# Four layers of cross attention on one core: last block projected into rows, its last sums on TensorE, small inputs fetched another way

## The chip, the cores and the metric

The kernel runs on one core of a Trainium2 chip. The metric is the device time of one execution in microseconds (us); before the change it was 4903.22 us, the median of three runs that lie between 4901.65 and 4903.43.

## The reference, cut to what matters

A sequence `x` of 2048 rows of 256 values goes through four layers of cross attention to the same context of 1601 rows of 512 values. Everything is float32. Layers 0, 2 and 3 are "masked" layers of 16 heads of 64 values; layer 1 is a grouped layer with an RMS norm ahead of it, which the change does not touch. A masked layer is, in the reference's words:

```python
q, k, v = hidden @ Wq, ctx @ Wk, ctx @ Wv            # 16 heads of 64
logits = einsum('bhqd,bhkd->bhqk', q, k) * 64 ** -0.5
col_bias[:, token_indices_A] = (-20.0 * (1 - mask_A))[:, None]
col_bias[:, token_indices_B] = (-20.0 * (1 - mask_B))[:, None]
out = softmax(logits + col_bias) @ v
hidden = out @ Wo + bo + hidden
```

`mask_A` and `mask_B` have one value for each of the 2048 rows, the token indices two values each, `bo` 256 values.

## The kernel before, in words

**Tiling.** A masked layer is done in 8 blocks of two heads. A block is done in four units, one for each quarter `b` of the rows (512 rows). A unit takes the context in 13 chunks of 128 positions (the last has 65); a step of the main loop (L1145) is one chunk. `x` is held transposed in `xs`: 256 columns as two groups of 128 partitions, rows along the free dimension.

**A unit.** Per chunk, TensorE makes the scores of both heads (L687) in a pair of PSUM banks, of which there are two (`psum.pair`), ScalarE copies them to SBUF (L699) and VectorE keeps a running maximum (L702, L704). After 13 chunks the maximum is turned (L747, L748), sent through DRAM to all partitions, and copied into a third PSUM pair `b` (L763). A unit later, per chunk, VectorE adds it (L768), ScalarE takes the exponential (L773), GpSimd adds the exponentials up in `sums` (a copy for chunk 0, L776, then twelve additions, L778), and TensorE multiplies them with the values (L813) into `po`, which ScalarE copies to `oT` (L818). Three pieces of work follow: `denominators` (L824) turns `sums` with eight transposes (L834), reduces (L838) and takes the reciprocal (L839), and sends the result through DRAM to all partitions as `by` (L655, L658); `divide` (L853) multiplies `oT` by it on GpSimd; `project` (L856) multiplies with `Wo` (L862) and adds to `xs` (L874), in the last block of a layer with the bias `bo` as well (L869). In the last block of the last layer `rows_out` (L626) then turns the quarter of `xs` back into rows with eight transposes (L631), copies it with ScalarE and VectorE, half each (L634, L635), and asks for two output transfers (L637).

**Order.** TensorE, ScalarE and VectorE run in the order in which the program is written (L1196 to L1202 make that binding). GpSimd and SyncE run in an order that the tile scheduler makes. Where the three pieces of a unit come is set by steps: `finish` (L876) gives the distance in steps from the unit's last chunk (2 or 3 for the denominators, 5 for the division, 10 for the projection), `after` (L1049) adds `rows_out` at 11. Projections of keys and values for the next block fill the steps between; in the last block there are none.

**Start.** `token_numbers` (L142) fetches twelve token indices, each to all 128 partitions, in six transfers of two values. Some 25 small VectorE instructions (`key_order`, L159) work out from them in which order the context rows are taken, and 13 indirect transfers of GpSimd gather the rows (L258). TensorE meanwhile turns `x` (L592) and makes the first queries (L464). `masks_parts` (L298) fetches both masks with row `n * 128 + p` on partition `p`, and the masks become bias rows later (L306 and on). `small_constants` (L370) fetches the biases `bo` and the norm's weights, value by value onto partitions, on GpSimd's queue; it is written at step 14 of the first unit, and the scheduler puts its requests at the start.

Of the kernel before, what the change touches and what calls it, by code (L numbers as in the profile page):

```python
# [10 lines left out]
FP = mybir.dt.float32  # L11
BF = mybir.dt.bfloat16
I32 = mybir.dt.int32
AF = mybir.ActivationFunctionType
ALU = mybir.AluOpType
# [3 lines left out]
P = 128  # L19
QB = 512  # L20
# [6 lines left out]
Piece = namedtuple("Piece", "run cost shared", defaults=(True,))  # L27
# [7 lines left out]
def tile_cross_attention_stack(ctx: ExitStack, tc: tile.TileContext, t: dict, out: bass.AP):  # L35
# [31 lines left out]
    nc = tc.nc  # L67
    x, cond = t["x"], t["ctx_2048"]
    _, S, C = x.shape
    _, T, CT = cond.shape  # L70
    NQ = S // P
    NC = C // P
    NCT = CT // P
    NB = S // QB
    QT = QB // P
    TCH = spans(T, P)
    NT = len(TCH)
# [3 lines left out]
    masked_names = ["L0_xattn_", "L2_xattn_", "L3_xattn_"]  # L81

    NP = 22
    const = ctx.enter_context(tc.tile_pool(name="const", bufs=1))
    weights = ctx.enter_context(tc.tile_pool(name="weights", bufs=2))
    heads = ctx.enter_context(tc.tile_pool(name="heads", bufs=2))
    probs = ctx.enter_context(tc.tile_pool(name="probs", bufs=NP))
    work = ctx.enter_context(tc.tile_pool(name="work", bufs=2))
    small = ctx.enter_context(tc.tile_pool(name="small", bufs=2))
    dram = ctx.enter_context(tc.tile_pool(name="dram", bufs=1, space=bass.MemoryType.DRAM))  # L90
    ps_o = ctx.enter_context(tc.tile_pool(name="ps_o", bufs=1, space=PSUM))
    ps_m = ctx.enter_context(tc.tile_pool(name="ps_m", bufs=1, space=PSUM))
    scores_pools = ctx.enter_context(ExitStack())

    ident = const.tile([P, P], FP, name="ident")
    make_identity(nc, ident)
    ones = const.tile([P, P], FP, name="ones")
# [32 lines left out]
    psum = Scores()  # L130
# [3 lines left out]
    xs = const.tile([P, NB, NC, QB], FP, name="xs")  # L134
# [5 lines left out]
    NTOK = 4 * NL  # L140

    def token_numbers():  # L142

        idx = const.tile([P, NTOK], I32, name="tok_idx")
        for l, name in enumerate(masked_names):
            for s, which, queue in ((0, "A", nc.sync), (2, "B", nc.scalar)):
                queue.dma_start(
                    out=idx[:, 4 * l + s : 4 * l + s + 2],
                    in_=t[name + "token_indices_" + which]
                    .rearrange("(o s) -> o s", o=1).to_broadcast((P, 2)),  # L150
                )
        tok = const.tile([P, NTOK], FP, name="tok")
        nc.vector.tensor_copy(tok, idx)
        wrap = small.tile([P, NTOK], FP, name="wrap", bufs=1)
        nc.vector.tensor_scalar(wrap, tok, 0.0, float(T), ALU.is_lt, ALU.mult)
        nc.vector.tensor_tensor(tok, tok, wrap, ALU.add)
        return tok
# [138 lines left out]
        nc.vector.tensor_copy(put(2), rest)  # L296

    def masks_parts():  # L298
        masks = probs.tile([P, 2, NQ], FP, name="p")
        with nc.allow_non_contiguous_dma(reason="2048 values of a mask, once"):  # L300
            nc.sync.dma_start(out=masks[:, 0, :], in_=t["mask_S_fk1"].rearrange("(n p) -> p n", p=P))
            nc.sync.dma_start(out=masks[:, 1, :], in_=t["mask_S_fk0"].rearrange("(n p) -> p n", p=P))
        parts = const.tile([P, 6, NQ], FP, name="mask_parts")

        def make():
            nc.vector.tensor_scalar(masks, masks, -1.0, 1.0, ALU.mult, ALU.add)  # L306
            nc.vector.tensor_scalar(masks, masks, -SUPPRESS, None, ALU.mult)
            for m in range(2):
                three_parts(masks[:, m, :], [NQ], lambda i: parts[:, 3 * m + i, :])

        return parts, make
# [52 lines left out]
    bo_of = []  # L364
# [5 lines left out]
    def small_constants():  # L370
        with nc.allow_non_contiguous_dma(reason="columns of 256 values"):
            for name in masked_names:
                bo_of.append(const.tile([P, NC], FP, name="bo_" + name))
                nc.gpsimd.dma_start(out=bo_of[-1], in_=t[name + "bo"].rearrange("(k p) -> p k", p=P))
            nc.gpsimd.dma_start(out=normw, in_=t["L1_xattn_norm_w"].rearrange("(k p) -> p k", p=P))
        nc.gpsimd.memset(sel, 0.0)
        for h, r in enumerate(QUARTERS):
            nc.gpsimd.tensor_copy(den_rows[:, h : h + 1], ident[:, r + 16 : r + 17])
            nc.gpsimd.tensor_copy(
                sel[:, :, h, :16], ident[:64, :64].rearrange("p (g d) -> p g d", d=16)  # L380
            )
        nc.vector.tensor_reduce(one_row, den_rows, AX.X, ALU.add)
# [240 lines left out]
            (12, Piece(rms, 1.5)),  # L623
        ]

    def rows_out(b):  # L626

        pt = psum.pair((QT, C))
        for q in range(QT):
            for k in range(NC):  # L630
                nc.tensor.transpose(pt[:, q, ts(k, P)], xs[:, b, k, ts(q, P)], ident)  # L631
        rows = work.tile([P, QT, C], FP, name="ct", bufs=3)
        half = QT // 2
        nc.scalar.copy(rows[:, :half, :], pt[:, :half, :])  # L634
        nc.vector.tensor_copy(rows[:, half:, :], pt[:, half:, :])  # L635
        for q0 in (0, half):
            nc.sync.dma_start(  # L637
                out=out[0, b * QB + q0 * P : b * QB + (q0 + half) * P, :].rearrange(
                    "(n p) c -> p n c", p=P
                ),  # L640
                in_=rows[:, q0 : q0 + half, :],
            )

    def columns(q):

# [15 lines left out]
    class Unit:  # L661
        def __init__(self, l, u, b, sub):
            self.l, self.u, self.b, self.sub = l, u, b, sub
            self.layer = u.layer
            self.pair = self.layer.SUBS[sub]
            self.masked = isinstance(self.layer, Masked)
            self.p = [None] * NT

        def rows(self, h):
            size = P // len(self.pair)  # L670
# [99 lines left out]
        def masked_exp(self, c):  # L770
            m = TCH[c][1]
            p = self.p[c]
            nc.scalar.activation(p[:m], p[:m], AF.Exp)  # L773
            if c == 0:
                self.sums = work.tile([P, 2, QB], FP, name="sums")
                nc.gpsimd.tensor_copy(self.sums, p)  # L776
            else:
                nc.gpsimd.tensor_tensor(self.sums[:m], self.sums[:m], p[:m], ALU.add)  # L778

        def scores_again(self, c, h, s):  # L780
# [17 lines left out]
        def values(self, c, part=None):  # L798


            u = self.u
            _, m = TCH[c]
            if c == 0 and not part:
                self.po = ps_o.tile([P, QB], FP, name="po")
            for h in range(len(self.pair)):
                r = self.rows(h)
                if self.masked:
                    to, v, p = self.po[r, :], u.v[:m, c, r], self.p[c][:m, h, :]
                else:
                    at = ts(part, QB // 2)  # L810
                    to, v = self.po[r, at], u.v[:m, c, :]
                    p = self.p[c][h // 2][:m, h % 2, at]
                nc.tensor.matmul(  # L813
                    to, v, p, start=(c == 0 and not part), stop=(c == NT - 1 and part != 0)
                )
            if c == NT - 1 and part != 0:
                self.oT = work.tile([P, QB], FP, name="oT", bufs=1)
                nc.scalar.copy(self.oT, self.po)  # L818

        @property  # L820
# [35 lines left out]
        def project(self):  # L856

            k = 0
            for py in psum.heads(False):
                of = range(k, k + py.shape[1])  # L860
                for k in of:
                    nc.tensor.matmul(  # L862
                        py[:, k - of[0], :], self.u.wo[:, ts(k, P)], self.oT, start=True, stop=True
                    )
                k += 1
                if self.masked and self.u.n == self.layer.BLOCKS - 1:
                    for j in of:
                        bo, to = bo_of[self.layer.l][:, j : j + 1], xs[:, self.b, j, :]
                        nc.vector.scalar_tensor_tensor(  # L869
                            to, py[:, j - of[0], :], bo, to, ALU.add, ALU.add  # L870
                        )
                else:
                    to = xs[:, self.b, of[0] : k, :]
                    nc.vector.tensor_tensor(to, py, to, ALU.add)  # L874

        def finish(self):  # L876

            last = 10 if self.masked else 8
            return [
                (2 if self.masked else 3, Piece(self.denominators, 1.0, not self.masked)),  # L880
                (5, Piece(self.divide, 0.0)), (last, Piece(self.project, 2.0, False)),
            ]
# [14 lines left out]
    units = []  # L897
# [118 lines left out]
    def start_block(i):  # L1016

        if i + 1 == len(blocks):
            return
        l, n = blocks[i + 1]  # L1020
        layer = layers[l]
# [27 lines left out]
    def after(k):  # L1049

        i, b, _ = units[k]
        l, n = blocks[i]
        if n + 1 < layers[l].BLOCKS or not of[k].last:
            return []
        if l + 1 == len(layers):
            return [(11, Piece(lambda: rows_out(b), 1.0))]
        if isinstance(layers[l + 1], Masked):
            return [(11, Piece(lambda: keep(l + 1, b), 0.0))]
        return norm_factors(l + 1, b)
# [176 lines left out]
```

## Time and profile before

| what | value |
|---|---|
| median of 3 runs | 4903.22 us |
| the profiled execution's own time | 4898.06 us |
| its span, first to last instruction | 4896.4 us |
| TensorE, VectorE, ScalarE, GpSimd busy | 97%, 77%, 66%, 61% of the span |
| mean granted TensorE clock | 0.981 of full |
| last unit: GpSimd copies chunk 0 at | 4842.58 us |
| last unit: matmuls of its last two chunks into `po` | 4868.44 to 4870.38 us |

The times in the views are counted from the start of the span. In a line of the timeline the first number is the start of a run of like instructions, the second the time from its start to its end; then come the engine, the source line, the operation, the tiles written and read, the shapes, the number of instructions in the run, and in brackets how long the engine was idle before and what ended that. An engine name with a `q` (SPq, ACTq) is the queue on which a transfer is asked for.

### The profile page before, as it was taken

What the parts mean: (1) busy time and instruction counts of PE and PEld (TensorE: products, weight loads), DVE (VectorE), ACT (ScalarE), POOL (GpSimd) and SP (SyncE); (2) the same over time, 40 slices, a digit from 0 to 9 for tenths busy, and PEclk for the clock granted to TensorE, in tenths of its full rate; (3) what the DMA queues carried; (4) which work ended last, traced back from release to release, by engine and by line L of the source; (5) the groups of instructions that cost most, each with busy time, mean ns of one, the idle gap of its engine ahead of it and who ended that gap; (6) DMA issues with size and microseconds to landing.
All of it is one profiled execution on the core that took longest, in us unless ns stands there. A gap on an engine that the chain in (4) does not pass through costs nothing.

```text
span 4896.4 us, 64042 instructions
## 1 busy us (share of the span) xinstructions
PE 4727.9 (97%) x24004; PEld 2059.7 (42%) x24004; DVE 3746.8 (77%) x3766; ACT 3221.9 (66%) x3994; POOL 2993.3 (61%) x1440
## 2 busy tenths in 40 slices
PE   8999999999999999999999999999999999999996
PEld 4444444443444444454344444444444444444432
DVE  5888888888766565653578888888888888888886
ACT  4777777777545544544567777777777777777774
POOL 3777777778610000000377777777777777777787
PEclk9999999999989999999899999999999999999998
DMA  4222222222210000011132222222232222222201
GB/s 146 87 83 78 87 75 88 80 80 73 65 38 21 20 21 20 19 41 45 44 92 88 83 80 82 77 88 77 78 90 79 83 78 87 75 88 84 76 29 35
DMA packets 354053, 337.87 MB, mean 69 GB/s; under 512 B 120681, under 2 KB 309353, under 8 KB 353744
## 3 DMA queue, kind: packets, MB, share of 16 engines
q1 hardware_dynamic: 350048, 328.41, 22.9%
q8 instruction: 189, 3.10, 0.3%
q0 software_dynamic: 1152, 3.28, 0.2%
q10 hardware_dynamic: 2544, 2.10, 0.1%
q14 instruction: 120, 0.98, 0.1%
HBM read 318.89 MB, written 14.82 MB: 68 GB/s over the span
## 4 chain that ended last, share of the span: by engine, by line
PE 87%; DVE 10%; issue 1%; POOL 1%; ACT 1%; DMA 0%; POOLq 0%; SPq 0%; DVEq 0%; ACTq 0%
PE po L813 28%; PE s L687 19%; PE t L718 8%; PE pm L394 7%; PE pm L440 6%; PE s L862 4%; PE pm L464 4%; PE t L783 3%; DVE ntop L748 2%; DVE rden L838 2%; PE s L834 2%; DVE xs L874 2%; PE s L747 2%; DVE top L704 1%; POOL sums L778 1%
## 5 line engine op out<-in xcount | busy, mean ns | idle before, releaser
L778 POOL TENSOR_TENSOR sums<-sums,p 128x1024 f32<-128x1024 f32 (+1 forms) x1152 | 2727.9, 2368 | 739.2 <-ACT p L773 568.3
L699 ACT COPY p<-s 128x1024 f32<-128x1024 f32 (+1 forms) x1248 | 1235.4, 1014 | 663.6 <-PE s L687 578.6
L813 PE MATMUL po<-p,v 128*64 128x512 f32 (+3 forms) x8320 | 1507.3, 529 | 8.9 <-ACT p L773 5.9
L768 DVE TENSOR_TENSOR p<-p,b 128x1024 f32<-128x1024 f32 (+1 forms) x1248 | 1461.3, 1209 | 55.2 <-ACT b L763 52.9
L704 DVE TENSOR_TENSOR top<-s,top 128x1024 f32<-128x1024 f32 (+1 forms) x1056 | 1291.2, 1223 | 239.1 <-ACT p L699 175.7
L687 PE MATMUL s<-q,kT 64*128 64x512 f32 (+1 forms) x4992 | 1342.2, 631 | 86.7 <-DVE ntop L748 23.7
L773 ACT ACTIVATE p<-p 128x1024 f32<-128x1024 f32 (+1 forms) x1248 | 1254.6, 1057 | 45.7 <-DVE p L768 44.3
L813 PEld LDWEIGHTS po<-p,v 128*64 128x64 f32 (+3 forms) x8320 | 367.0, 126 | 1096.5 <-issue 864.4
L687 PEld LDWEIGHTS s<-q,kT 64*128 64x128 f32 (+1 forms) x4992 | 390.0, 182 | 725.6 <-issue 218.7
L795 ACT ACTIVATE p<-t 128x512 f32<-128x512 f32 (+1 forms) x760 | 412.2, 594 | 410.8 <-PE t L718 373.8
L731 DVE TENSOR_REDUCE row_top<-t 128x1 f32<-128x512 f32 x700 | 451.2, 686 | 256.5 <-PE t L718 253.1
L854 POOL TENSOR_TENSOR oT<-oT,by 128x512 f32<-128x512 f32 x112 | 143.3, 1280 | 758.8 <-DMA by<-cols 365.6
L718 PE MATMUL t<-kT,q 32*128 32x512 f32 (+1 forms) x1880 | 560.5, 639 | 0.0
L783 PE MATMUL t<-q,kT 32*128 32x512 f32 (+1 forms) x1520 | 491.6, 659 | 0.0
L718 PEld LDWEIGHTS t<-kT,q 32*128 32x128 f32 x1880 | 295.4, 316 | 167.6 <-issue 83.3
L394 PEld LDWEIGHTS pm<-wv,ct 128*128 128x128 f32 (+1 forms) x2600 | 300.4, 187 | 130.3 <-issue 66.9
L394 PE MATMUL pm<-wv,ct 128*128 128x128 f32 (+2 forms) x2600 | 333.3, 281 | 2.2 <-ACT v L398 0.9
L440 PE MATMUL pm<-ct,wk 128*128 128x256 f32 (+1 forms) x1344 | 314.6, 377 | 2.7 <-issue 2.7
L440 PEld LDWEIGHTS pm<-ct,wk 128*128 128x128 f32 x1344 | 230.7, 190 | 157.9 <-issue 100.1
L748 DVE TENSOR_REDUCE ntop<-s 128x8 f32<-128x1024 f32 x96 | 117.6, 1225 | 232.7 <-PE s L747 232.7
L862 PE MATMUL s<-oT,wo 128*128 128x512 f32 x392 | 199.1, 631 | 16.2 <-POOL oT L854 12.5
L776 POOL COPY sums<-p 128x1024 f32<-128x1024 f32 x96 | 99.7, 1039 | 183.6 <-ACT p L773 183.6
(149 smaller groups left out, 2308.0 us busy)
## 6 DMA issues: line engine op xcount, KB each, us to landing
ct<-ctxT SPq DMA_DIRECT2D x288, 512.0 KB
xT<-xT SPq DMA_DIRECT2D x100, 512.0 KB
spread<-cols SPq DMA_DIRECT2D x96, 512.0 KB
by<-cols SPq DMA_DIRECT2D x192, 128.0 KB
xT<-xs SPq DMA_DIRECT2D x16, 512.0 KB
ct<-ctxT SPq DMA_DIRECT2D x48, 130.0 KB
wk<-in_L_xattn_Wk_dram SPq DMA_DIRECT2D x24, 256.0 KB
wv<-in_L_xattn_Wv_dram SPq DMA_DIRECT2D x24, 256.0 KB
```

Of the source, the lines that this page charges most:

```text
L394: nc.tensor.matmul(pv[:md, d, :f], ct(k)[:, d * P : d * P + md], wv[:, k, :], start=(k == 0), stop=(k == NCT - 1),)
L440: nc.tensor.matmul(pk, u.wk[:, k, :], ct(k), start=(k == 0), stop=(k == NCT - 1))
L687: nc.tensor.matmul(s[:m, h, :], self.u.kT[r, a : a + m], self.q[r, :], start=True, stop=(a != TAIL),)
L699: nc.scalar.copy(p[:m], s[:m])
L704: nc.vector.tensor_tensor(self.top[:m], s[:m], self.top[:m], ALU.max)
L718: nc.tensor.matmul(s[:, at : at + n], self.q[r, columns(q)], self.u.kT[r, a : a + n], start=True, stop=True,)
L731: nc.vector.tensor_reduce(self.top[:, of, q, k : k + 1], s, AX.X, ALU.max)
L768: nc.vector.tensor_tensor(self.p[c][:m], self.p[c][:m], self.less[:m], ALU.add)
L773: nc.scalar.activation(p[:m], p[:m], AF.Exp)
L778: nc.gpsimd.tensor_tensor(self.sums[:m], self.sums[:m], p[:m], ALU.add)
L783: nc.tensor.matmul(s[:m], self.u.kT[r, a : a + m], self.q[r, :], start=True, stop=True)
L813: nc.tensor.matmul(to, v, p, start=(c == 0 and not part), stop=(c == NT - 1 and part != 0))
```

## The change

It has two parts.

**The start.** The token indices go to one partition; a VectorE copy turns them to float, and one matmul of a row of ones with them puts them on all partitions. The masks are fetched as 32 rows of 128 values and turned by one transpose. The tiles of `bo` and of the norm's weights are set to zero by VectorE, where `small_constants` is written, before they are fetched, so that the requests wait for that.

**The last block.** Rows instead of columns: for the first three quarters `x` is turned into rows early in the last block (`rows_of_x`, at steps 2, 12 and 38 of it), and `project_rows` multiplies with `oT` as the stationary side, so that rows come out, adds the rows of `x` and asks for the two output transfers. The bias `bo` of the last layer is added a block earlier, in `project` of block 6. For the very last unit, GpSimd adds up chunks 0 to 5 only; chunks 6 to 12 and `sums` go through matmuls with a matrix of ones into `dens`, which gives the denominators on all 64 partitions of each head, without the way through DRAM. `x_below` puts the last quarter's rows of `x` into four PSUM banks by matmuls with the identity, and `quarters` does the reciprocal, the division (GpSimd), the projection on top of `x`, a copy and an output transfer for each 128 rows. The denominators and the division of the third quarter come at 4 and 7 steps instead of 2 and 5, and its `project_rows` runs inside `quarters`.

```diff
 def token_numbers():
-        idx = const.tile([P, NTOK], I32, name="tok_idx")
+        idx = small.tile([1, NTOK], I32, name="tok_idx", bufs=1)
...
-                    .rearrange("(o s) -> o s", o=1).to_broadcast((P, 2)),
+                    in_=t[name + "token_indices_" + which].rearrange("(o s) -> o s", o=1),
+        row = small.tile([1, NTOK], FP, name="tok_row", bufs=1)
+        nc.vector.tensor_copy(row, idx)
+        pt = ps_m.tile([P, NTOK], FP, name="pm")
+        nc.tensor.matmul(pt, ones[:1, :], row, start=True, stop=True)
-        nc.vector.tensor_copy(tok, idx)
+        nc.vector.tensor_copy(tok, pt)
...
 def masks_parts():
-            nc.sync.dma_start(out=masks[:, 0, :], in_=t["mask_S_fk1"].rearrange("(n p) -> p n", p=P))
-            nc.sync.dma_start(out=masks[:, 1, :], in_=t["mask_S_fk0"].rearrange("(n p) -> p n", p=P))
+            nc.sync.dma_start(
+                out=rows[m * NQ : (m + 1) * NQ, :], in_=t[name].rearrange("(n p) -> n p", p=P)
+            )
...
+            nc.tensor.transpose(
+                pt.rearrange("p m n -> p (m n)"), rows, ident[: 2 * NQ, : 2 * NQ]
+            )
...
 def small_constants():
+                nc.vector.memset(bo_of[-1], 0.0)
                 nc.gpsimd.dma_start(out=bo_of[-1], in_=t[name + "bo"].rearrange("(k p) -> p k", p=P))
+            nc.vector.memset(normw, 0.0)
...
+    def rows_of_x(b):
+                nc.tensor.transpose(pt[:, q, ts(k, P)], xs[:, b, k, ts(q, P)], ident)
+        x_rows_of[b] = work.tile([P, QT, C], FP, name="ct", bufs=3)
+        nc.scalar.copy(x_rows_of[b], pt)
...
 def masked_exp(self, c):
-            else:
+            elif c < self.added:
                 nc.gpsimd.tensor_tensor(self.sums[:m], self.sums[:m], p[:m], ALU.add)
...
 def values(self, c, part=None):
+            if self.masked and self.very_last:
...
+                        nc.tensor.matmul(
+                            self.dens[self.rows(h), :], ones[:k, :64], p[:k, h, :],
+                            start=(c == self.added), stop=(p is self.sums),
+                        )
...
+        def project_rows(self, py=None):
+            for q in range(QT):
+                nc.tensor.matmul(
+                    py[:, q, :], self.oT[:, ts(q, P)], self.u.wo, start=True, stop=True
+                )
+            rows = x_rows_of[self.b]
+            nc.vector.tensor_tensor(rows, py, rows, ALU.add)
+            for q in (0, QT // 2):
+                rows_out(self.b, rows, q, QT // 2)
...
+        def x_below(self):
+            for q in range(QT):
+                for k in range(NC):
+                    nc.tensor.matmul(
+                        self.py[q][:, ts(k, P)], xs[:, self.b, k, ts(q, P)], ident,
+                        start=(k == 0), stop=False,
+                    )
...
+        def quarters(self, before):
+            for q in range(QT):
+                nc.vector.reciprocal(rden[:, ts(q, P)], self.dens[:, ts(q, P)])
+                nc.gpsimd.tensor_tensor(
+                    self.oT[:, ts(q, P)], self.oT[:, ts(q, P)], rden[:, ts(q, P)], ALU.mult
+                )
+            before.project_rows(psum.b().rearrange("p a (b c) -> p (a b) c", c=C))
+            rows = work.tile([P, QT, C], FP, name="ct", bufs=3)
+            for q in range(QT):
+                nc.tensor.matmul(
+                    self.py[q], self.oT[:, ts(q, P)], self.u.wo, start=False, stop=True,
+                )
+                nc.scalar.copy(rows[:, q, :], self.py[q])
+                rows_out(self.b, rows, q, 1)
...
 def start_block(i):
         if i + 1 == len(blocks):
+            for b, at in enumerate((2, 12, 38, NB * NT + 12)):
+                piece = Piece(lambda b=b: rows_of_x(b), 1.0, False)
+                if b == NB - 1:
+                    piece = Piece(lambda: of[len(units) - 1].x_below(), 2.0, False)
+                pieces.at(start + at, [(0, piece)])
```

## The prediction

> **What bounds the kernel now.** I read the page first, then the timeline and the windows of the first 60 us, the timeline and the chain of the last 100 us, the groups by form for durations, and the order of the built program on each engine, before and after.
>
> ```profile
> PE 4727.9 (97%) x24004; PEld 2059.7 (42%) x24004; DVE 3746.8 (77%) x3766; ACT 3221.9 (66%) x3994; POOL 2993.3 (61%) x1440
> ...
> PE 87%; DVE 10%; issue 1%; POOL 1%; ACT 1%; DMA 0%; POOLq 0%; SPq 0%; DVEq 0%; ACTq 0%
> ```
>
> TensorE is the bound, and the middle of the program is the same instructions in the same order before and after. So only the ends can pay: what the start takes until TensorE runs without holes, and what follows the last work that fills TensorE. The timeline of the end:
>
> ```profile
> 4844.15 17.06 POOL L778 TENSOR_TENSOR sums<-sums,p 128x1024 f32<-128x1024 f32 x7 [0.53 <-ACT p L773]
> ...
> 4861.16 1.26 POOL L854 TENSOR_TENSOR oT<-oT,by 128x512 f32<-128x512 f32 x1
> 4862.38 12.04 POOL L778 TENSOR_TENSOR sums<-sums,p 128x1024 f32<-128x1024 f32 x5
> ...
> 4874.47 1.98 PE L834 MATMUL s<-ident,sums 128*128 128x128 f32 x8 [4.09 <-POOL sums L778]
> 4876.49 1.23 DVE L838 TENSOR_REDUCE rden<-s 128x8 f32<-128x1024 f32 x1 [6.64 <-PE s L834]
> ...
> 4883.32 1.26 POOL L854 TENSOR_TENSOR oT<-oT,by 128x512 f32<-128x512 f32 x1 [8.90 <-DMA by<-cols]
> 4884.64 3.78 PE L862 MATMUL s<-oT,wo 128*128 128x512 f32 x4 [8.18 <-POOL oT L854]
> ...
> 4889.92 1.76 PE L631 MATMUL s<-ident,xs 128*128 128x128 f32 x7 [0.18 <-DVE xs L869]
> ...
> 4892.34 0.69 DVE L635 COPY ct<-s 128x512 f32<-128x512 f32 x1 [2.47 <-ACT ct L634]
> ```
>
> GpSimd's twelve additions of the last unit end at 4874.42; from there a serial path of 22 us (transposes, reduce, DRAM, divide, project, add, turn, copy, output) runs with every engine idle between. The exponentials were done at about 4859.3 (4850.32 + 8.97, L773). The start:
>
> ```profile
> 7.82 0.17 DVE L153 CAST tok<-tok_idx 128x12 f32<-128x12 int32 x1 [4.36 <-DMA tok_idx<-ttn_token_indices_A_dram]
> ...
> 11.65 4.47 SPq L302 DMA_DIRECT2D p<-in_mask_S_fk_dram  x1
> ...
> 14.62 1.52 POOL L258 DMA_INDIRECT p<-in_ctx_dram,src_rows  x1 [7.25 <-DVE src_rows L239]
> ```
>
> ```profile
> 10.00:15.00 5.00, 3.73 (x10) 2.20 (x9) 4.62 (x21) 2.29 (x2) 0.38 (x1) 1.00 1.11 340
> 15.00:20.00 5.00, 5.00 (x24) 3.81 (x23) 4.80 (x9) 2.19 (x3) 4.02 (x4) 1.00 1.15 190
> 20.00:25.00 5.00, 1.81 (x14) 1.31 (x13) 2.65 (x17) 2.44 (x3) 3.79 (x4) 1.00 0.96 314
> 25.00:30.00 5.00, 4.21 (x16) 3.32 (x14) 0.00 (x0) 0.00 (x0) 3.79 (x4) 0.66 0.89 339
> 30.00:35.00 5.00, 2.46 (x6) 1.19 (x8) 0.00 (x0) 1.72 (x3) 4.16 (x13) 0.74 1.04 410
> 35.00:40.00 5.00, 5.00 (x32) 3.69 (x29) 1.23 (x1) 3.07 (x4) 0.00 (x0) 0.92 0.95 334
> ```
>
> The chain is token indices, VectorE, gathers; the DMA engines (share before the last column) are full until 40 us; TensorE has holes of 2.72 and 3.33 us and a low clock, and runs without a hole from 36.05.
>
> **What the Trainium skill says.** "DMA: Bandwidth & Descriptors", Rules for kernel authors: a strided last dimension becomes a descriptor per element. The trace agrees: 5673 of 13650 packets in the first 60 us are under 512 B; the masks are 4096 of them. Same page, Anatomy of one DMA: about 2.0 us fixed per transfer (fitted for GpSimd's path). Here the last index request is made at 1.8 and its data are awaited 5.93 us. "VectorE: DVE Perf Modes", first hardware budget: the reciprocal repeats 8 times. The trace agrees in kind: 178, 203 and 258 ns for 4, 8 and 16 columns, 6.9 ns a column. "TensorE: Matmul & The Clock Gate", Part 1: idle windows of 3.4 us halve the clock. Here the last 17 us ran at 0.50.
>
> **The end, part by part.** Removed for the last unit: seven additions (7 x 2.37 us), L834, L838, the DRAM trip (4877.98 to 4883.3), L862, L869, L631, L634/L635. Added on TensorE: 7 + 1 groups of denominator matmuls and `x_below`. They are of the shape of L813 (64 columns, 512 rows, two heads side by side), where eight instructions, two chunks, take 1.94 us: 0.97 us a group. `x_below` is 16 passes like L394's 16 in 1.95 us.
>
> TensorE of the last unit starts when `oT` is copied, 4840.96 before; L634 (0.57) ahead of that copy is gone, so matmuls start near 4841.0 instead of 4841.6. Then 13 x 0.97 values, 1.24 for L834 of the third quarter, 8 x 0.97 denominators, 1.95 `x_below`: 23.6, so 4864.6. Does something else come later? VectorE: 12 additions at 1.13 spacing and 1.43 for L838/L839 from 4839: 4854; exponentials 4857. GpSimd: copy at 4842.58, five additions: 4855.7; `by` of the third quarter (rden near 4849, trip 5.3) 4854.3, division to 4857. All before TensorE needs them; TensorE is the new last.
>
> After 4864.6: four reciprocals of 128 columns, not in the trace: 0.203 + 120 x 0.0069 = 1.03 each (low bound 0.26, a plain 128-column pass; high 1.3), so 4.1; they hide the third quarter's `project_rows` (1.7 to 3.4). Then the last GpSimd quarter 0.46 (2.368 and 1.28 us for 1024 and 512 columns give 0.19 + 0.0021 a column), its matmul 0.5, copy 0.37 (L441's size), four hand-overs 0.2: 4870.2. Queued behind the last quarter's output on SP are the third quarter's two, so three requests at 0.55: 4871.9. Before, the last request ended near 4893.5 and the span at 4896.4, 2.9 later. New end 4874.8: **-21.6 us**. Bounds: -23 with quick reciprocals and full clock; -13 if the two heads' ones-matmuls do not run side by side (+7.6) and the clock halves.
>
> **The last block before that.** The first quarter's way through L862, L869, L631, L634 was on the chain from 4799.46 to 4805.15, 5.7 us; now project and one addition, 1.96 + 1.22: -2.5. Added inside the block are three times eight transposes (1.09) and a ScalarE copy (1.01 instead of 0.58) that take a turn of the two PSUM pairs; scores behind them wait for the copy. Two of the three were in the end before. Between 4700 and 4840 TensorE and VectorE are both some 90% busy, so 0.5 to 3 us each; I take 1.1: +3.3. L869 twice (1.49) for L874 (1.22) in block 6, four times 0.27: TensorE covers it there (39.2 of 40 us busy), at most +1.1, taken 0.2. Sum **+1**, from -2 to +6.
>
> **The start, part by part.** Six transfers of 128 pieces become six of one piece. With the page's 2 us after the last request the indices land near 4.3; copy 0.17, a 12-column matmul (L843's 4 columns took 0.38), copy 0.17: `tok` near 5.2 instead of 7.99: -2.8 on the chain to L239 and the first gather; GpSimd is free then, since its four bias requests (3.2 us) are gone from there. The token matmul is first on TensorE; behind it are the transposes of `x`, which waited for data until 9.49: costs nothing unless indices land after 9. Masks: 4096 pieces of some 10 ns in the trace's packet records, over 16 engines 2.6 us of all DMA, and 4.5 us of SP ahead of L596; now 32 pieces. Their transpose stands before the first context transposes (20.22 before), asked for at about 7, ahead of three weight transfers of 0.4 us each: nothing, up to 1. Biases: four memsets (at most 0.17 each, L98) after 88.87 on VectorE, ahead of L344; 0 to 0.7, taken 0.3. Their requests then sit on GpSimd near 89 to 92.5, ahead of L776 at 98.45: hidden by 6 us. If gathers come 2.8 earlier and DMA has 2.6 us less to move, the TensorE holes shrink; what is late next is `x`, whose transposes end at 20.4. From -2.5 (the chain alone) to -9 (both holes and the half-clock windows beside them gone). I take **-5**.
>
> **Sum** against the execution's own 4898.06: -21.6 + 1 - 5 = -25.6, 4872.5. The median of the runs is 5.2 above that execution, so 4877.6; I say 4878.
>
> **Rivals.**
> - A, as worked out: 4878. Chance 0.61.
> - B, the start gives nothing: gathers and `x` share full DMA engines, so earlier requests land no earlier. For: share 0.89 to 1.15 throughout. Against: 4096 pieces are gone. 4883. Chance 0.13.
> - C, the start loses both holes: 4878 - 4 = 4874. For: the low clock beside the holes. Chance 0.12.
> - D, the turned `x` costs the block more: three turns at 3 us, and heads one after the other at the end: 4878 + 6 + 5 = 4889. Chance 0.06.
> - E, it does not do what it says: GpSimd's division still waits for the third quarter's trip, which queues the end as before; only the start and the DRAM trip of 5.3 us gain, 4892 to 4896. Against: the trip starts before 4850. Chance 0.04.
> - F, slower: the granted clock. Its mean is 0.981, low in the grouped layer's short waits; an earlier start moves every one of those against the clock's windows. 25.6 us is 0.52% of the span, so a mean under 0.976 turns the sign; 0.970 gives 4878 + 54 = 4932. For: nothing in the trace says what the shift does. Against: the runs lie within 1.8 us. Chance 0.04.
>
> Within 0.2% of before, some 9.8 us, is about what a measurement here can tell from no change. Below 4893.4 are A to D and half of E: 0.94; within 0.2%: 0.03; slower: 0.03. Range 4868 to 4888: A with its bounds, B and C; D, E, F and the tails are left out.
>
> **What would show it.** Right: span near 4871; no L834 of the last unit; seven runs of ones-matmuls among L813's in the last 25 us with TensorE busy; reciprocals of about 1 us; span end some 10 us after the last ones-matmul; the first gather near 11.8; steady TensorE from about 31. Wrong: reciprocals hidden by something longer, TensorE waiting for GpSimd's division, holes in the first 36 us of the same size, or a mean clock other than 0.98.

## The result, and the profile after

| kernel | median, us | its runs, us | ratio to before, 95% interval |
|---|---|---|---|
| before | 4902.48 | 6, 4901.25 to 4903.43 | |
| changed | 4872.05 | 6, 4864.09 to 4876.59 | 0.9936 [0.9923, 0.9949] |

The change takes 30.4 us off, 0.64%; 25 were forecast. The profiled execution of the changed kernel took 4865.5 us (span 4863.4, mean granted clock 0.984); that of before took 4898.06.

The page of the changed kernel, the lines that answer to the first lines shown of before, busy time by engine and the shares of the chain that ended last:

```profile
PE 4721.2 (97%) x24055; PEld 2058.6 (42%) x24055; DVE 3745.7 (77%) x3768; ACT 3223.6 (66%) x3997; POOL 2979.2 (61%) x1436
...
PE 87%; DVE 10%; ACT 1%; issue 1%; POOL 1%; DMA 0%; DVEq 0%; ACTq 0%; SPq 0%; POOLq 0%
```

Little moves in these totals: TensorE is the bound of both. The gain is in the ends. The timeline of the changed kernel, its end:

```profile
4830.29 5.13 PE L832 MATMUL po<-p,v 128*64 128x512 f32 x20 [0.82 <-ACT oT L854]
...
4834.74 12.23 POOL L797 TENSOR_TENSOR sums<-sums,p 128x1024 f32<-128x1024 f32 x5
...
4838.27 1.03 PE L845 MATMUL pm<-p,ones 128*64 128x512 f32 x4
...
4839.23 2.05 PE L930 MATMUL s<-ident,xs 128*128 128x128 f32 x16
...
4849.85 1.03 PE L832 MATMUL po<-p,v 65*64 65x512 f32 x4
...
4850.71 1.03 PE L845 MATMUL pm<-p,ones 65*64 65x512 f32 x4
...
4851.57 1.03 PE L845 MATMUL pm<-sums,ones 128*64 128x512 f32 x4
4852.53 1.99 PE L916 MATMUL b<-wo,oT 128*128 128x256 f32 x8
4852.64 3.39 DVE L939 RECIPROCAL xT<-pm 128x128 f32<-128x128 f32 x4 [7.83 <-PE pm L845]
...
4855.39 4.86 SPq L651 DMA_DIRECT2D out_dram<-ct  x6
...
4857.87 0.37 ACT L949 COPY ct<-s 128x256 f32<-128x256 f32 x1 [0.85 <-PE s L946]
```

GpSimd's five additions are over at 4846.97. TensorE goes on with groups of values (L832) and groups of ones (L845), 0.86 us apart, until 4852.6; the reciprocals start right there. Before, 22 us of one engine after another followed GpSimd's last addition; now 11 us follow the last group of ones. The start:

```profile
3.33 0.20 DVE L153 CAST tok_row<-tok_idx 1x12 f32<-1x12 int32 x1 [0.83 <-DMA tok_idx<-ttn_token_indices_B_dram]
...
4.22 0.17 DVE L157 COPY tok<-pm 128x12 f32<-128x12 f32 x1 [0.69 <-PE pm L155]
...
11.04 1.67 POOL L262 DMA_INDIRECT p<-in_ctx_dram,src_rows  x1 [7.23 <-DVE src_rows L243]
...
24.68 1.99 PE L706 MATMUL s<-q,kT 64*128 64x512 f32 x8
```

and the windows of the start (busy time of PE, PEld, DVE, ACT, POOL, then the clock, the DMA share and GB/s), where before had TensorE busy for 1.81 and 4.21 us in the same two:

```profile
20.00:25.00 5.00, 3.90 (x26) 3.22 (x25) 2.46 (x15) 2.23 (x4) 3.80 (x4) 1.00 0.93 336
25.00:30.00 5.00, 5.00 (x31) 3.53 (x28) 1.23 (x1) 3.60 (x5) 4.30 (x7) 1.00 1.04 411
```

The first gather is asked for 3.6 us earlier, and TensorE is without a hole from 21.89 instead of 36.05.

**Where the time went.** Both kernels calculate a maximum per unit (`ntop`), in the same order; its 96 times in the masked layers are markers along both traces. Changed minus before, in the two profiled executions: -9.5 us at the first marker, -9.1 after the grouped layer, -9.9 before the last block, -9.0 at the last unit's marker, -33.0 at the end. So the start gave 9.5, the middle about nothing, the last block cost 0.9, the end gave 24.0. The forecast had -5, 0, +1, -21.6. The question of the experiments was the start: is 9.5 us real?

### The profile page after: what moved, and what is told of

Same layout as the page of the kernel before. It is cut to its first block, busy times and chain, and to the rows that moved or that the text cites. A ratio compares the mean times of both kernels' runs of the same rounds, so it can differ in the third digit from the quotient of the medians.

```text
span 4863.4 us, 64146 instructions
## 1 busy us (share of the span) xinstructions
PE 4721.2 (97%) x24055; PEld 2058.6 (42%) x24055; DVE 3745.7 (77%) x3768; ACT 3223.6 (66%) x3997; POOL 2979.2 (61%) x1436
## 3 DMA queue, kind: packets, MB, share of 16 engines
q1 hardware_dynamic: 345158, 328.14, 23.6%
## 4 chain that ended last, share of the span: by engine, by line
PE 87%; DVE 10%; ACT 1%; issue 1%; POOL 1%; DMA 0%; DVEq 0%; ACTq 0%; SPq 0%; POOLq 0%
PE po L832 28%; PE s L706 19%; PE t L737 8%; PE pm L406 6%; PE pm L452 6%; PE pm L476 4%; PE s L898 4%; PE t L802 3%; DVE rden L874 2%; DVE ntop L767 2%; PE s L870 2%; DVE xs L910 2%; PE s L766 2%; DVE top L723 1%; DVE p L787 1%
## 5 line engine op out<-in xcount | busy, mean ns | idle before, releaser
L797 POOL TENSOR_TENSOR sums<-sums,p 128x1024 f32<-128x1024 f32 x1145 | 2712.4, 2369 | 740.0 <-ACT p L792 569.6
L832 PE MATMUL po<-p,v 128*64 128x512 f32 (+3 forms) x8320 | 1505.9, 529 | 4.9 <-ACT p L792 2.6
L832 PEld LDWEIGHTS po<-p,v 128*64 128x64 f32 (+3 forms) x8320 | 367.1, 126 | 1090.5 <-issue 866.9
L890 POOL TENSOR_TENSOR oT<-oT,by 128x512 f32<-128x512 f32 x111 | 142.0, 1279 | 750.3 <-PE t L737 249.9
L782 ACT COPY b<-spread 128x1024 f32<-128x1024 f32 x96 | 97.5, 1016 | 149.8 <-DVE p L787 149.7
L898 PE MATMUL s<-oT,wo 128*128 128x512 f32 x376 | 187.8, 622 | 3.3 <-DVE row_top L750 1.7
```

The source lines that it names most:

```text
L832: nc.tensor.matmul(to, v, p, start=(c == 0 and not part), stop=(c == NT - 1 and part != 0))
```

## The experiments

The theories when they began were about the start: that the chain of the token indices gives the gain (T1 in the expectations), against the DMA room of the masks' 4096 pieces (T2) and the place of the bias requests (T3). When the first four runs gave nothing at all, the question became where it goes: that the granted clock, which drops to half speed for stretches in the grouped layer, moves a run by as much as the start gains (W), against causes in the start itself: its holes belong to one execution (R) or to the kernel (H).

### The start alone, and its three parts

Before, with `token_numbers`, `masks_parts` or the two memsets of `small_constants` taken from the changed kernel, or all three:

```diff
-        idx = const.tile([P, NTOK], I32, name="tok_idx")
+        idx = small.tile([1, NTOK], I32, name="tok_idx", bufs=1)
...
-            nc.sync.dma_start(out=masks[:, 0, :], in_=t["mask_S_fk1"].rearrange("(n p) -> p n", p=P))
+                out=rows[m * NQ : (m + 1) * NQ, :], in_=t[name].rearrange("(n p) -> n p", p=P)
...
+                nc.vector.memset(bo_of[-1], 0.0)
```

All three:

> The start of the change alone, the last block as before. Marker: the first values' sixteen matmuls, at 38.65 us before and 29.30 with the whole change. If both ends act on their own: marker near 29.3 and the time 9 us under the kernel before (4893.5). If the earlier start is partly eaten later in the grouped layer: 3 to 6 us under.

The indices:

> Only the token indices go to one partition and through the matmul; masks and biases as before. Theory T1 (the chain from the indices to the gathers sets the start): the first gather near 11.0 instead of 14.62, marker at 30 to 32, time 7 to 9 us under before. Theory T2 (the masks' 4096 pieces fill the DMA engines and hold gathers and x): first gather near 11.5, marker only 3 us earlier (35.5), time 3 us under before.

The masks:

> Only the masks are fetched as rows and turned by a transpose; indices and biases as before. T1: first gather at 14.6 as before, marker 37 to 38.6, time 0 to 2 us under before. T2: first gather at 14.6, but both TensorE holes (2.72 and 3.33 us) gone, marker at 32 to 33, time 5 to 6 us under before.

The biases:

> Only the biases and norm weights are asked for later. T1 and T2: nothing, marker 38.0 to 38.7, time within 1 us. Theory T3 (the four requests keep GpSimd or the DMA engines from the gathers): marker 2 us or more earlier.

| part | median, us (runs) | ratio, interval | first gather at | first values matmuls at |
|---|---|---|---|---|
| none (before, measured with them) | 4900.33 (63) | | | |
| all three | 4898.59 (20) | 1.0004 [0.9995, 1.0013] | 11.04 | 28.36 |
| indices | 4895.38 (12) | 0.9996 [0.9985, 1.0007] | 12.12 | 28.20 |
| masks | 4902.19 (20) | 1.0010 [1.0001, 1.0020] | 14.73 | 31.90 |
| biases | 4900.39 (20) | 1.0004 [0.9994, 1.0015] | 14.51 | 30.96 |

The runs of before lie between 4882.50 and 4904.64. No part makes the kernel measurably faster, and all three don't together; the intervals exclude the 9 and the 3 to 6 us expected of all three, and the 5 to 6 that T2 expected of the masks. For the indices alone the interval reaches from 7.4 us less to 3.4 more, too wide to tell T1's 7 from T2's 3 by the time. But the traces show an effect in its place: with the indices changed, the first gather is 2.5 to 3.6 us earlier and the first values matmuls come at 28.2 or 28.4. With the masks or the biases alone the first gather stays at 14.5 to 14.7 (before: 14.62), and the values matmuls come at 31 to 32, where the next section finds them in before as well. So T1 has the right place, and the masks and the biases give nothing. The gain is lost later: in the execution profiled with all three parts, the markers are 10.4 us ahead of before's at the start, 10.0 at the last marker ahead of the grouped layer, 0.1 at the first one behind it, 1.1 before the last block, and 2.8 behind at the last unit's marker. The last block loses its 3.9 beside a stretch of 10.2 us at half clock at 4695, which before does not have there. Neither the layer nor the block was edited.

### The same kernels once more

Both kernels unchanged, on one chip.

> The kernel before, unchanged, for a second profile of it. Theory R (the holes of 2.72 and 3.33 us in the first profile's start belong to that one execution): first gather near 14.6, the first values' sixteen matmuls near 31.5 instead of 38.76, as in the runs with one part of the start changed (31.9 with the masks alone, 31.0 with the biases alone). Theory H (the holes belong to the kernel): marker at 38 to 39 again. Theory W (the granted clock in the grouped layer makes two groups of run times): times in two groups, near 4883 at a mean clock of 0.983 and near 4901 at 0.978.

> The changed kernel, unchanged, on the same chip as the kernels beside it, for many times of both. R: its start is worth 3 to 4 us, its end 24, together 27 to 28 at the same granted clock. H: 33 at the same clock. W: times scatter over some 12 to 18 us in line with the mean clock, and at equal clock the difference to before is constant.

Measured: before 4901.01 us (12 runs, 4886.38 to 4903.81; 0.9997 [0.9988, 1.0005]), the changed kernel 4874.76 (4 runs, 4861.48 to 4876.40; 0.9939 [0.9920, 0.9958]). They scatter by 17 and 15 us, along with the mean clock: before takes 4886 to 4892 where it is 0.980 to 0.982, and 4899 to 4904 at 0.978 or 0.979; the changed kernel took 4861.48 at 0.985 and 4873 to 4876 at 0.981. At the same mean clock of 0.981 the two differ by 12 to 19 us (before takes 4888 to 4892 there), not by the 27 to 28 or 33 expected: in before, 33 us of the end are at half clock, much of that with TensorE idle (busy for 6.01 of the last 17 us), in the changed kernel 5 or 6, so the mean does not compare the two kernels. The windows of before, second execution, at the start:

```profile
20.00:25.00 5.00, 3.58 (x23) 2.85 (x21) 2.71 (x17) 2.39 (x3) 3.79 (x4) 1.00 1.01 314
25.00:30.00 5.00, 4.58 (x24) 2.77 (x23) 0.46 (x1) 3.31 (x4) 3.79 (x4) 1.00 0.93 286
```

and its timeline of TensorE:

```profile
26.41 1.99 PE L687 MATMUL s<-q,kT 64*128 64x512 f32 x8
28.32 1.99 PE L440 MATMUL pm<-ct,wk 128*128 128x256 f32 x8
30.16 1.04 PE L271 MATMUL b<-ident,p 128*128 128x128 f32 x8
31.03 1.95 PE L394 MATMUL pm<-wv,ct 128*128 128x128 f32 x16
```

The same program that had TensorE busy for 1.81 us between 20 and 25 is busy for 3.58 there, and its first values matmuls come at 31.03, not 38.76. The holes of 2.72 and 3.33 us on which the prediction built its rival C belong to one execution, not to the kernel. 7.7 of the 9.5 us were those holes (R, not H). Against this execution the changed kernel's two are ahead by 1.7 and 2.0 us (29.30 and 29.05). And the grouped layer, the same code in all four traces (the column before the DMA share is the granted clock):

The windows of the changed kernel, second execution:

```profile
1250.00:1400.00 150.00, 135.60 (x568) 62.66 (x569) 99.52 (x104) 57.71 (x71) 66.39 (x36) 0.80 0.19 54
1400.00:1900.00 500.00, 500.00 (x3864) 238.37 (x3861) 292.96 (x481) 248.45 (x455) 17.01 (x25) 0.95 0.09 24
```

The windows of the changed kernel, first execution:

```profile
1250.00:1400.00 150.00, 135.48 (x584) 65.34 (x584) 104.51 (x106) 62.41 (x75) 75.29 (x40) 0.84 0.21 61
1400.00:1900.00 500.00, 500.00 (x3912) 240.45 (x3908) 296.84 (x487) 250.91 (x460) 17.03 (x25) 0.97 0.08 24
```

In the second of these stretches TensorE is busy throughout in both, and starts 3864 matmuls at a clock of 0.95 and 3912 at 0.97. Added up from the clock's record, half-speed stretches within the grouped layer are 153.6 us in the first execution of the changed kernel and 180.9 in the second; 150.2 and 139.9 in the two of before, 180.9 with the start alone. They are multiples of 3.4 us. By the markers, the two executions of the changed kernel are 0.9 us apart at the last marker ahead of the grouped layer and 11.3 at the second one behind it, and stay so to the last; the two of before are 7.0 and 13.0 apart there, and 9.1 after the last block, where the second has 10.2 us at half clock at 4756. Such a scatter hides a gain of 3.

### Both kernels without the grouped layer

That is the test: where that layer is gone, the scatter should go, and the change's own gain should be left.

```diff
-    layers = [Masked(0), Grouped(), Masked(1), Masked(2)]
+    layers = [Masked(0), Masked(1), Masked(2)]
```

> The kernel before without its grouped layer 1 (three masked layers are left, so the output is another). W: the scatter of 20 us is gone, all times within 3 us, mean clock above 0.99. If the scatter has another cause: it stays.

> The changed kernel without its grouped layer 1, like its neighbour. Without the scatter the change's two ends show on their own: R: 27 to 28 us under the neighbour; H: 33 us under it.

Measured: 3835.00 us for before (4 runs, 3834.09 to 3836.53) and 3809.07 for the changed kernel (4 runs, 3807.94 to 3810.24): each scatters by 2.4 us or less, and their difference is 25.9, where R expected 27 to 28 and H 33. By the markers: first gather 15.77 to 10.81, first values matmuls 31.44 to 27.82 (-3.6), -1.7 before the last block, +1.0 within it, -25.3 from the last marker to the end, -26.0 in all. Four runs are few: the first six of before lay within 2.2 us with the layer. But the markers above agree, so W holds in the main: most of the scatter of 15 us is made in the grouped layer, and the last block can add 3.9. Why the clock drops there is not shown. The start is worth 3.6 us at its place in this pair (1.7 and 2.0 against the second execution of before), and of that 1.7 is left at the last block. In this execution of before the first gather came 1.1 us later than in the other two.

### What the ends are made of

Three kernels without the grouped layer and one whole one, measured together on another chip (before has a median of 4903.29 us there). First, the last unit's sums left to GpSimd:

```diff
-    LAST_ADDED = 6
+    LAST_ADDED = 13
...
-                            start=(c == self.added), stop=(p is self.sums),
+                            start=True, stop=True,
```

> The changed kernel without layer 1 (another output), and GpSimd adds up all thirteen chunks of the last unit; TensorE's ones-matmuls take the finished sum alone. If the seven chunks on TensorE are about half of the end's gain: GpSimd's sum ends 29.3 us after its copy, 12 to 13.5 us later than TensorE is done now, and the time is 12 to 13.5 us over the changed kernel without layer 1 (3821 to 3823). Rival, the DRAM trip and the turning were most of the gain: under 6 us over (below 3815).

Then two of the turns of `x` two steps later, in the next unit, behind the transposes of the maximum:

```diff
-            for b, at in enumerate((2, 12, 38, NB * NT + 12)):
+            for b, at in enumerate((2, 14, 40, NB * NT + 12)):
```

> The changed kernel without layer 1, with the second and third turn of x two steps later (steps 14 and 40 instead of 12 and 38), so that they stand behind and not ahead of the transposes of the running maximum. Theory: the place costs, since at the last step of a unit VectorE waits for those transposes: 2 to 3.3 us under the changed kernel without layer 1 (3806 to 3807). Rival: a turn costs its PSUM pair and ScalarE copy anywhere: within 0.5 us.

Then that with one group of ones less, the last four projections on alternating PSUM banks, and the third quarter's output in one request on ScalarE's queue:

```diff
-    LAST_ADDED = 6
+    LAST_ADDED = 7
...
-            self.py = [pairs[q // 2][:, q % 2, :C] for q in range(QT)]
+            self.py = [pairs[q % 2][:, q // 2, :C] for q in range(QT)]
...
+                late.append(lambda: rows_out(self.b, rows, 0, QT, nc.scalar))
```

> Like the one with the later turns, and besides GpSimd adds up chunk 6 as well (TensorE six chunks), the four quarters' banks alternate between the two pairs so that a quarter's matmul doesn't wait for the copy of the one before, and the third quarter's rows go out in one request on ScalarE's queue. Theory: TensorE is last at the end, so 0.9 us for the chunk, 0.5 for the banks, 1.0 to 1.4 for the output queue: 2.4 to 2.8 us under the kernel with the later turns alone. Rival, the reciprocals and GpSimd's quarters are last: 1.0 to 1.9 us.

| kernel | median, us | its runs, us |
|---|---|---|
| sums on GpSimd | 3836.74 | 4, 3834.11 to 3840.33 |
| later turns | 3821.37 | 4, 3818.86 to 3823.95 |
| later turns and a shorter end | 3820.98 | 4, 3819.22 to 3822.27 |

All three are more than 10 us above what was expected, and the trace says where. The timeline of TensorE with later turns, at the start:

```profile
19.33 1.09 PE L275 MATMUL b<-ident,p 128*128 128x128 f32 x8
30.01 3.78 PE L452 MATMUL pm<-ct,wk 128*128 128x256 f32 x8 [9.59 <-ACT ct L277]
```

and its chain that ended last, in that place:

```profile
21.17 1.00 ACT xs L605
22.17 6.78 issue
28.95 1.02 ACT ct L277
```

ScalarE sits for 6.78 us ahead of a copy whose transposes ended near 20.4 by the records, and the chain names no work that it waits for. All three of these kernels have it in their profiles (first values matmuls at 38.8 to 39.4, where the changed kernel without the layer had 27.82), though their code is the same as that kernel's up to the last block. They are 10.9 to 11.9 us late at the first markers. The first execution of before had holes in the same place. What makes it stays open: up to 25 us the DMA engines are as full in the execution without it (shares of 0.95 to 1.00, against 0.91 to 1.01). One profile shows one execution, but the medians lie about as high, so most of the unprofiled runs of these three seem to have it; the whole kernel measured with them, below, has little of it (31.7).

So the three are compared with each other, at the markers of the traces. Later turns gain 0.96 us at the last marker against the kernel with the early ones (sums on GpSimd), where 2 to 3.3 were expected, and under 0.5 by the rival: neither number is met; the place of a turn costs something, but less than thought. The rest of what the block lost there against the earlier chip is 3 to 4 us beside a half-speed stretch of 10.2 us at 3717, which all three kernels have and the earlier one hasn't.

Sums on GpSimd cost 15.4 us from the last marker to the end (61.4 against 45.9 with later turns), or 16.5 against the changed kernel without the layer on the earlier chip (44.9), where 12 to 13.5 were expected. Its timeline:

```profile
3817.13 7.17 POOL L797 TENSOR_TENSOR sums<-sums,p 128x1024 f32<-128x1024 f32 x3
3824.36 1.98 PE L845 MATMUL pm<-sums,ones 128*64 128x512 f32 x4 [17.93 <-POOL sums L797]
3826.26 3.78 PE L916 MATMUL b<-wo,oT 128*128 128x256 f32 x8
```

TensorE has nothing to do for 17.93 us, and finds its clock halved when it has: the same four matmuls take 1.98 us instead of 1.03, the next eight 3.78 instead of 1.99. So 15.4 to 16.5 of the end's 25.3 us go with the chunks that TensorE adds up, the clock's part in them included. The other 9 to 10 are a difference: rows, quarters and the way through DRAM, which no run separates.

The shorter end gains 1.5 us from the last marker on (45.93 to 44.48; 0.4 by the medians) where 2.4 to 2.8 were expected. The rival's 1.0 to 1.9 fits the number but not its reason: the reciprocals come 0.8 earlier, the price of a group of ones (0.86), and the last copy another 0.5, which fits the banks. Of the 1.0 to 1.4 for the requests there is 0.1. The timeline of the shorter end:

```profile
3813.45 2.71 SPq L651 DMA_DIRECT2D out_dram<-ct  x4
...
3815.49 0.40 ACTq L651 DMA_DIRECT2D out_dram<-ct  x1
```

SyncE's requests end at 3816.16 instead of 3819.07, but the span ends at 3820.2. By the trace's packet records the whole quarter, asked for at 3815.49 on ScalarE's queue, and the quarters on SyncE's queue are moved until the same time, 3818.45 and 3818.48: SyncE's last packet ends 2.3 us after its last request, not 1.7 as with later turns.

The whole changed kernel with these edits:

> The whole changed kernel (with layer 1) with the later turns, six chunks on TensorE, alternating banks and the output on ScalarE's queue. At equal granted clock 4 to 6 us under the changed kernel: 4869 to 4871 at a clock of 0.981, 4857 at 0.985.

Measured: 4879.48 us (5 runs, 4875.02 to 4881.38), 0.9954 [0.9933, 0.9975], at clocks of 0.980 and 0.981: 4 us or more above what was expected. It doesn't beat the changed kernel (0.9936 and 0.9939, whose intervals overlap with it). Against the second execution of that one (on the earlier chip), its trace is 2.8 us later at the first markers, level after the grouped layer, 0.9 earlier in the last block and 0.5 in the end, in which a half-speed stretch of 3.4 us falls at 4841. The edits gain 1.4 us in their places, and one start or one window more is worth more than that.

## Why the prediction was right, point by point

**The end, forecast -21.6, measured -24.0** (-25.3 without the grouped layer). The mechanism is the forecast's: TensorE is last, GpSimd's additions and the division lie beside it, the DRAM trip is gone. The stretch from the last unit's first values matmuls to the end of the span was to take 33.8 us (4841.0 to 4874.8) and took 33.1 (4830.29 to 4863.4). Its terms, mis-sized in both directions:

- A group of four matmuls was priced at 0.97, from two chunks in 1.94 us. In a run of groups they start 0.86 apart. TensorE's 23.6 us became 22.3. That the two heads' ones-matmuls run side by side, doubted in the bounds, is shown by their starts: in the group at 4842.12 two start 0.007 us apart, the next two 0.43 later; four matmuls over the full width with the same 512 rows (L898, at 4678.55) take 1.96 us, these four 1.03. The Trainium skill, "TensorE: Matmul & The Clock Gate", Part 3, describes matmuls in separate tiles of the array that run concurrently; the trace agrees.
- A reciprocal of 128 columns was extrapolated to 1.03 us and takes 0.82 (3.39 for four with the waits between them).
- The three last requests were to end 1.65 us after the last copy; they end 2.0 after (4858.24 to 4860.25), and the span 3.2 after that, not 2.9.

That is 0.7 us of the 2.4 by which the end gained more than forecast. The remaining 1.7 lie ahead of it: the last unit starts at 4830.29, where the shift of -9.0 at its marker would put it at 4832.0. The second and third quarters' work that is gone from there is the likely reason, but no run separates it.

**The last block, forecast +1, measured +0.9, and +1.0 without the grouped layer.** Marker by marker: +2.3 at the first, +0.2, +1.0 and then -2.6. The last fits the -2.5 for the first quarter's way, which lay in that stretch. (The division of the first two quarters, too, comes at 7 steps instead of 5; no run separates that.) The three turns at 1.1 each are right in sum only. The timeline of the changed kernel around the second:

```profile
4707.48 1.09 PE L643 MATMUL s<-ident,xs 128*128 128x128 f32 x8
...
4708.41 1.12 PE L766 MATMUL s<-ident,top 128*128 128x128 f32 x8
4708.64 1.00 ACT L645 COPY ct<-s 128x1024 f32<-128x1024 f32 x1
4709.57 1.23 DVE L767 TENSOR_REDUCE ntop<-s 128x8 f32<-128x1024 f32 x1 [2.39 <-PE s L766]
```

The turn (L643) stands ahead of the transposes of the maximum (L766), and VectorE idles for 2.39 us until these are done. The timeline of before in the same place:

```profile
4717.17 1.23 DVE L748 TENSOR_REDUCE ntop<-s 128x8 f32<-128x1024 f32 x1 [1.58 <-PE s L747]
```

So the turn is on the chain of `ntop`, for 0.8 us, not only in the queue for the PSUM pairs. The third (4781.46, with L766 at 4782.39) stands the same way and has the same 2.39; the first, at 4677.13, doesn't. Two steps later neither stands there: the idle time is back at 1.57 in both places, and 0.96 us come back at the last marker.

**The start, forecast -5, from -2.5 to -9.** This is the step that was off, though by the first two profiles it was only too small (-9.5). What it has beyond -2.5 was read off the masks' pieces and one execution of before, whose holes of 2.72 and 3.33 us were not there in the next. What the kernel gains at the first values matmuls is 1.7 to 3.6 us, about the chain alone, for which the range's small end, -2.5, would have been right: the indices landed by 3.33, at most 1.5 us after their last request ended (4.3 forecast, with 2), `tok` at 4.22 (5.2 forecast, 7.99 before), first gather 11.04 (11.8 forecast, 14.62 before). That the token matmul costs nothing is right: it runs at 3.58, and TensorE waits for `x` until 6.44. Of the masks' 2.6 us of DMA time nothing is seen: with them alone the first gather is at 14.73. Why the pieces cost nothing is not shown. The biases, taken at 0.3 from 0 to 0.7, cost the whole 0.7: from the first marker to the second it takes 34.0 us with them (the changed kernel, all three parts, the changed kernel without the layer) and 33.3 without (before, indices alone, masks alone). That is too little for the medians (1.0004 [0.9994, 1.0015]).

**The sum, -25.6.** Without the grouped layer it is -26.0, and by the medians of that pair -25.9. Two errors of 1.4 to 3.7 us, the end too small and the start too large, cancel; that the sum is this close is luck. In the whole kernel the medians differ by 30.4 in the first set and by about 26 in the second (4901.01 and 4874.76); what lies between is within the scatter that the clock makes. The first median, 4872.05, lies nearer to rival C's 4874 than to 4878, but not for C's reason.

**Rival F, the granted clock,** is real as a scatter, but made no loss here: runs of one and the same kernel lie up to 22 us apart with it (4882.50 to 4904.64 for before). The prediction's argument against it, that three runs of before lay within 1.8 us, was worth little. E falls: GpSimd's division (L890) is done at 4848.2, four microseconds before its result is read. B and C are both answered by the second execution of before: the start gives something, and the holes weren't the kernel's to lose. D's 3 us a turn is not reached: +2.3 at the first marker, with two turns ahead of it.

## What to carry to other kernels

When an end is queued behind one engine's reductions, ask whether the engine that feeds it can do the last of them itself: eight groups of ones on TensorE at 0.86 us each (seven chunks and the sum) replaced seven additions at 2.37 and a way through DRAM. Before a hole in a profile goes into a sum, look for it in a second execution of the same kernel; a hole that the chain puts down to no work may not be the kernel's. Where the clock swings in one stage, measure a small gain with that stage taken out: the runs of one kernel spread over 2.3 to 6.2 us there (five kernels, four runs each), and over 15 to 22 with it. Then compare markers along two traces: they say in which stage a difference arose.

## What the runs showed of the hardware

- The granted clock falls to half for multiples of 3.4 us in the grouped layer, at places that differ between executions of one program: 140 to 181 us of it in all, and run times of 4883 to 4904 us for before that go with mean clocks of 0.983 to 0.978. It can also fall in the last block, for 10.2 us (4695 with all three parts of the start, 4756 in the second execution of before), beside a loss of 3.9 us. What sets it off is not shown. The Trainium skill, "TensorE: Matmul & The Clock Gate", Part 1, says that the activity window runs free of the kernel, so that the slow matmuls at a kernel's start differ from run to run; these traces show such a difference in the middle of a kernel, and its 0.4% of the time is enough to cover or feign a change of this size.
- A start that is the same code takes until 27.8 or until 39.4 us to its first values matmuls; neither the first gather (10.8 in both) nor the share of the DMA engines up to 25 us tells the two apart.
- Six small transfers of the token indices to one partition had landed by 3.33 us (3.10 in the second execution); the same values to 128 partitions each were awaited until 7.70.
- The same two runs of matmuls take 1.98 and 3.78 us after 17.93 us without work, and 1.03 and 1.99 where TensorE was busy before.
